# A convolution and whitening kernel: a DRAM buffer with rows p and 128+p of an image side by side

## The chip, the cores and the metric

The kernel runs on one core of a Trainium2 chip. The metric is device time in microseconds (us). Before the change, three runs gave 902.69, 903.47 and 903.47 us, median 903.47. A profiled execution is a run of its own; its span reaches from its first to its last instruction.

## The reference

The input x holds 4 images of 64 channels of 256 x 256 float32 pixels (67.1 MB). Two layers follow.

```
# layer 0: per channel a long 2-D convolution, kernel = outer product of two generated 1-D filters
k = einsum('ijk,imk->ijmk', hx, hy)
y = irfft2(rfft2(x, 512 x 512) * rfft2(k, 512 x 512) / 512)[..., :256, :256] + x * bias

# layer 1: whitening over the 64 channels
x1  = y as (64, 4*65536)
s   = x1[:, ::9]                       # every ninth pixel
mean = mean(s);  cov = s @ s.T / n + 0.01 * I
out = inverse_sqrt(cov, 5 Newton-Schulz steps) @ (x1 - mean)
```

The convolution is causal in both image directions and separable, so it is computed as two products with triangular Toeplitz matrices. The whitening matrix needs a sample of every image before the first output pixel can be made, so y has to be kept in full in the meantime: it goes out to DRAM and comes back.

## The kernel before

**First stage, the convolution.** The 64 channels are worked in groups of CG = 8; a step is one group g of one image n, 32 steps in all. The order of the steps is written out by hand (`steps`): the first six groups go through all four images, then the last two groups image by image, so that image 0 is complete after step 25, image 1 after step 27, and so on. A step's input sits in one of four tiles of [128 partitions, 8 channels, 2, 256], partition p holding the image rows p (index b = 0) and 128 + p (b = 1) of each channel. The tile is loaded two channels at a time (`load_x`, L101, 512 KB each) two steps ahead. `group` computes two channels' second product beside the next two channels' first one (L220, TensorE), ScalarE copies the first product out of PSUM (L409), VectorE adds the bias term and writes y over x in the tile (L412). Then `store` sends the two channels to DRAM (L425), in two transfers, one for each b, and VectorE picks the sample out of the tile (L319).

**The buffer in DRAM.** `y_d[n]` has H2 * C = 128 rows of 32768 floats: row b * 64 + channel, and in it the 128 image rows of half b one after another. A store of two channels and one b writes, from each of the 128 partitions, one run of 256 floats (1 KB) for each channel.

**The reload.** The last stage works in 32 pieces (n, q), eight for an image. A piece is a tile of [128, 4096], 2 MB: partition b * 64 + channel, 4096 consecutive floats of that row of `y_d[n]`. `load_y` (L357) loads it in one transfer of 128 runs of 16 KB. The tiles are placed, by the list `homes`, in thirteen buffers of the pools that the first stage leaves free; a piece's load waits until its buffer's earlier user is done. Nine loads are put by hand into the last steps of the first stage (`early`), the first after step 26's third quarter; four follow at its end. Piece i + 13 is loaded once the output store of piece i has left the buffer.

**Whitening.** After the last step the sample's covariance is summed (L333), and `whitening` computes the 64 x 64 matrix W and the shift: a short chain of small products.

**Last stage.** For each piece, four blocks: W times 64 partitions of 512 columns, four matmuls into two PSUM banks (L635), one bank evacuated by ScalarE (L639), the other by VectorE (L640), both in place over the piece's tile. The two column runs of a block lie 2048 apart (`v` splits the 4096 columns in two halves). Then the piece goes out (L645): piece 0 in four stores, piece 1 and the last two in two each, all others in one of 2 MB. GpSimd (POOL) issues the stores of pieces 1 to 18, SP those of piece 0 and of pieces 19 to 31. The order of pixels within the output tensor is settled on the host by a transpose.

**What sets the order.** Engines run their instructions in the order in which the kernel is written. SP issues nearly all transfers: x loads, Toeplitz loads (L193), y stores, y loads and some of the output stores, in one queue. A transfer that has to wait there, for a semaphore or for room, holds up all that is written behind it. Within a step SP's order for two channels is: y store, x load, Toeplitz load if any, y load if any.

Of the kernel before, what the change touches and what calls it, by code (L numbers as in the profile page):

```python
# [38 lines left out]
F32 = mybir.dt.float32  # L39
I32 = mybir.dt.int32  # L40
AF = mybir.ActivationFunctionType
ALU = mybir.AluOpType
# [3 lines left out]
NB, C, L = 4, 64, 256  # L46
P, H2 = 128, 2
EMB, ORDER = 33, 64
PIX = L * L
CG = 8  # L50
# [7 lines left out]
FP = 4096  # L58
# [6 lines left out]
def conv_whiten_kernel(ctx: ExitStack, tc: tile.TileContext, a: dict, out: bass.AP):  # L65
    nc = tc.nc
# [8 lines left out]
    dram = ctx.enter_context(tc.tile_pool(name="dram", bufs=1, space=bass.MemoryType.DRAM))  # L75
    psA = ctx.enter_context(tc.tile_pool(name="psA", bufs=8, space=bass.MemoryType.PSUM))

    y_d = [dram.tile([H2 * C, PIX // H2], F32, tag=f"y{n}", name=f"y_d{n}") for n in range(NB)]
    g_d = dram.tile([P, GW], F32, tag="g", name="g_d")
    g0_d = dram.tile([2 * CG, GW], F32, tag="g0", name="g0_d")  # L80

# [6 lines left out]
    cols = const.tile([P, 4], F32, tag="cols", name="cols")  # L88
# [9 lines left out]
    bias = const.tile([P, C], F32, tag="bias", name="bias")  # L98
# [22 lines left out]
    for n in range(NB):  # L121
        t = spool.tile([P, FP], F32, tag="samp", name=f"samp{n}")
# [32 lines left out]
    for i in range(3):  # L155
        for u in range(2):
# [3 lines left out]
            arg, k, nxt = (scratch[:, 2 + 3 * i + v, half] for v in range(3))  # L160
# [152 lines left out]
    def pack_ops(g, n, yt, cs):  # L313
        def op(s):
            nj = (L - s + STEP - 1) // STEP
            src = yt[:, cs, :, s : s + STEP * (nj - 1) + 1 : STEP].rearrange("p c b j -> p b j c")
            dst = samp[n][:, :, 0:nj, g * CG + cs.start : g * CG + cs.stop]
            m = mask[:, n, :, s : s + 1].unsqueeze(3).to_broadcast([P, H2, nj, cs.stop - cs.start])
            nc.vector.copy_predicated(dst, m, src)  # L319

        cost = 0.3 + 1.5e-3 * H2 * NJ * (cs.stop - cs.start)
        return [(cost, lambda s=s: op(s)) for s in range(STEP)]
# [21 lines left out]
    pieces = [(n, q) for n in range(NB) for q in range(PIX // H2 // FP)]  # L344
# [7 lines left out]
    def load_y(i):  # L352

        n, q = pieces[i]
        pool, tag = homes[i % len(homes)]
        t = pool.tile([P, FP], F32, tag=tag, name=f"yi_{n}_{q}")
        nc.sync.dma_start(out=t, in_=y_d[n][:, q * FP : (q + 1) * FP])  # L357
        return t

    def load_next():  # L360
        loaded[len(loaded)] = load_y(len(loaded))
# [10 lines left out]
    for g in range(1, C // CG):  # L372
        first = 16 * g - 14 if g < C // CG - 1 else 16 * g - 22
        for part in range(8):
            k = first + (part * 12 // 8 if g < C // CG - 2 else part)
# [18 lines left out]
    def group(first, second):  # L394

        units = []
        g1, n1, c1, x1, o1s1 = first
        g2, n2, c2, x2, o1s2 = second
        for u in range(2):
            job2 = (bank(f"p2_{g2}_{n2}_{c2 + u}"), o1s2[u], toep[g2][:, 1, c2 + u, :])  # L400
            job1 = (bank(f"p1_{g1}_{n1}_{c1 + u}"), x1[:, c1 + u], toep[g1][:, 0, c1 + u, :])
            units.append((job1, job2))

        toeplitz_products(units, orders[0])
        orders.reverse()
        for u in range(2):
            o1 = o1pool.tile([P, H2, L], F32, tag="o1", name=f"o1_{g1}_{n1}_{c1 + u}")
            for to, fr in ((slice(0, HP), slice(HP, P)), (slice(HP, P), slice(0, HP))):
                nc.scalar.copy(o1[to], units[u][0][0][fr])  # L409
            o1s1.append(o1)  # L410
            ch = g2 * CG + c2 + u
            nc.vector.scalar_tensor_tensor(  # L412
                x2[:, c2 + u], x2[:, c2 + u], bias[:, ch : ch + 1], units[u][1][0],
                ALU.mult, ALU.add,
            )

        store(second)
        pack(2.92)

    def store(second):  # L420
        g, n, c, yt, _ = second
        halves = g >= C // CG - 2
        for b in range(H2):
            row = b * C + g * CG + c
            nc.sync.dma_start(  # L425
                out=y_d[n][row : row + 2, :].rearrange("c (p w) -> p c w", w=L),
                in_=yt[:, c : c + 2, b],
            )

        if c == CG - 2 and (g, n) != steps[-1]:  # L430
            todo.extend(pack_ops(g, n, yt, slice(CG // 2 if halves else 0, CG)))
        elif c == CG // 2 - 2 and halves:
            todo.extend(pack_ops(g, n, yt, slice(0, CG // 2)))
# [123 lines left out]
    with tc.manual_schedule(  # L557
# [9 lines left out]
        for i, (g, n) in enumerate(steps):  # L567
            xt = x_tiles[i % 4]
            for c in range(0, CG, 2):
# [19 lines left out]
                if (i, c) in blocks:  # L589
                    tg, part = blocks[i, c]  # L590
# [6 lines left out]
        g, n, c, yt, _ = pending[0]  # L597
        for item in pending:
            half_group(item, 1)
            pack(1.0)  # L600
            store(item)
# [13 lines left out]
        W, shift = whitening(i15, ones)  # L615


    halves = [slice(u * C, (u + 1) * C) for u in range(2)]
    for i, (n, q) in enumerate(pieces):
        yt = loaded.pop(i)  # L620

        v = yt.rearrange("p (v f) -> p v f", v=2)
        o = out[n, q].rearrange("p (v f) -> p v f", v=2)

        part = 512 if i == 0 else 1024 if i == 1 or i > len(pieces) - 3 else 2048
        for w in range(FP // 1024):


            cols = slice(w * 512, (w + 1) * 512)
            po = [  # L630
                psA.tile([P, 512], F32, tag="psA", name=f"po_{n}_{q}_{w}_{u}") for u in range(2)
            ]
            for k in range(2):
                for u in range(2):
                    nc.tensor.matmul(  # L635
                        po[u][halves[k]], lhsT=W[halves[u]], rhs=v[halves[u], k, cols],
                        start=True, stop=True,
                    )
            nc.scalar.activation(v[:, 0, cols], po[0], AF.Identity, bias=shift)  # L639
            nc.vector.tensor_scalar(v[:, 1, cols], po[1], shift, None, ALU.add)  # L640
            end = (w + 1) * 512
            if end % part == 0:

                issue = nc.sync if i == 0 or i + len(homes) >= len(pieces) else nc.gpsimd
                issue.dma_start(out=o[:, :, end - part : end], in_=v[:, :, end - part : end])  # L645
        if i + len(homes) < len(pieces):
            loaded[i + len(homes)] = load_y(i + len(homes))

# [57 lines left out]
```

## Time and profile before

| | |
|---|---|
| median of three runs | 903.47 us |
| span of the profiled execution | 902.1 us |
| TensorE busy (matmul) | 781.2 us, 87% |
| VectorE, ScalarE, GpSimd busy | 64%, 44%, 2% |
| bytes moved by DMA | 285.6 MB, 317 GB/s over the span |
| read from HBM, written to HBM | 149.35 MB, 134.44 MB |
| chain that ended last: TensorE | 74% (64% of it the convolution's products, L220) |
| same chain: DMA, with the steps whose releaser isn't known | 11% and 7% |
| first and last y load issued (L357) | 507.7 us, 829.1 us |
| convolution's last product ends | about 613 us |
| first product of the last stage (L635) | 643.3 us |

An issue table lists transfers by the line that issues them, with their size in KB and the median time from issue to landing. A DMA packet is a run of bytes that one of the core's 16 DMA engines moves in one go; the trace records its start, its duration and its size. A busy share of the DMA engines is a mean over the sixteen: two full engines and fourteen idle ones would show as 0.13. The chain that ended last is followed back from the last instruction to what released it, step by step.

### The profile page before, as it was taken

The page shows a single profiled execution, that of the slowest core. Times are in us where ns is not written, and L with a number is a line of the kernel's source. Part 1 is how long each engine was busy: PE and PEld are TensorE (multiplying, and loading weights), DVE is VectorE, ACT ScalarE, POOL GpSimd, SP SyncE. Part 2 cuts the span into 40 slices and gives each one's busy share as a digit, 9 for nine tenths or more (in the row PEclk, how much of TensorE's full clock was granted, in tenths as well). Part 3 has the DMA queues.
Part 4 walks back from the last instruction along what each step waited for, and adds up shares of the span by engine and source line. Part 5 has one row for each costly group of instructions (what it writes and reads, how often), then busy time and mean ns, then how long its engine had stood idle before and what let it go on. Part 6 is the DMA issues. An engine that isn't in the chain of part 4 may idle for free.

```text
span 902.1 us, 28046 instructions
## 1 busy us (share of the span) xinstructions
PE 781.2 (87%) x11928; PEld 647.5 (72%) x11928; DVE 581.5 (64%) x801; ACT 395.5 (44%) x676; POOL 14.5 (2%) x40
## 2 busy tenths in 40 slices
PE   8999999999999999999999999999999565666200
PEld 7999999999999999999999999999533111212000
DVE  3487778877888778877888877877688332233200
ACT  2655554545455555545454444442487232233200
POOL 1000000000000000000000000000010000000000
PEclk9999999999999999999999999999999766866755
DMA  7988889798788888888997899979999999999998
GB/s 209 327 262 252 242 261 271 234 273 251 247 263 261 244 264 259 258 250 267 293 275 241 285 351 356 335 237 390 375 401 429 430 432 432 429 434 430 430 430 355
DMA packets 117912, 285.61 MB, mean 317 GB/s; under 512 B 8891, under 2 KB 91116, under 8 KB 110108
## 3 DMA queue, kind: packets, MB, share of 16 engines
q1 hardware_dynamic: 113436, 244.94, 79.0%
q0 software_dynamic: 3056, 37.95, 10.0%
q8 instruction: 95, 1.56, 0.7%
q10 hardware_dynamic: 1296, 0.93, 0.4%
q14 instruction: 29, 0.24, 0.1%
HBM read 149.35 MB, written 134.44 MB: 315 GB/s over the span
## 4 chain that ended last, share of the span: by engine, by line
PE 74%; DMA 11%; another core or an unknown queue 7%; DVE 0%; issue 0%; SPq 0%; ACT 0%; POOLq 0%; DVEq 0%
PE p L220 64%; DMA out_dram<-yi 5%; DMA yi<-y_d 5%; PE po L635 4%; PE pc L333 2%; PE ph L252 1%; PE pk L300 1%; PE spin L442 1%; DMA toep<-g_d 0%; PE busy L152 0%; PE pm L158 0%; SPq L357 0%; DMA scratch<-in_zw_dram 0%; DVE yi L640 0%
## 5 line engine op out<-in xcount | busy, mean ns | idle before, releaser
L220 PE MATMUL p<-toep,x 64*64 64x64 f32 (+3 forms) x5040 | 579.5, 284 | 0.8 <-issue 0.8
L220 PE MATMUL p<-toep,o 64*64 64x64 f32 (+3 forms) x5040 | 579.5, 284 | 0.0
L220 PEld LDWEIGHTS p<-toep,x 64*128 64x128 f32 (+1 forms) x5040 | 535.7, 166 | 24.4 <-issue 1.3
L220 PEld LDWEIGHTS p<-toep,o 64*128 64x128 f32 (+1 forms) x5040 | 536.7, 166 | 10.7 <-issue 0.2
L409 ACT COPY o<-p 64x512 f32<-64x512 f32 x504 | 292.8, 581 | 294.2 <-PE p L220 286.6
L319 DVE COPY_PREDICATED samp<-mask,x 128x464 f32<-128x464 int32 (+3 forms) x351 | 297.2, 847 | 9.8 <-DVE x L412 0.2
L412 DVE SCALAR_TENSOR_TENSOR x<-x,bias,p 128x512 f32<-128x512 f32 x252 | 179.8, 744 | 121.3 <-PE p L220 117.3
L635 PE MATMUL po<-yi,chain 64*64 64x512 f32 x1024 | 143.7, 720 | 60.4 <-DMA yi<-y_d 60.4
L640 DVE TENSOR_SCALAR yi<-po,shift 128x512 f32<-128x512 f32 x128 | 96.1, 751 | 109.0 <-PE po L635 100.7
L635 PEld LDWEIGHTS po<-yi,chain 64*64 64x64 f32 x1024 | 48.0, 162 | 155.2 <-issue 150.5
L639 ACT ACTIVATE yi<-po,shift 128x512 f32<-128x512 f32 x128 | 88.0, 687 | 116.7 <-PE po L635 116.0
L333 PE MATMUL pc<-samp 128*64 128x65 f32 x464 | 14.9, 223 | 0.0
L333 PEld LDWEIGHTS pc<-samp 128*64 128x64 f32 x464 | 14.3, 137 | 0.3
L645 POOL DMA_DIRECT2D out_dram<-yi x19 | 10.5, 554 | 130.5 <-DMA out_dram<-yi 55.1
L606 POOL TENSOR_SCALAR chain<-ident 64x64 f32<-64x64 f32 x2 | 1.0, 519 | 606.6 <-PE ph L252 606.6
L286 DVE COPY o<-ph 64x256 f32<-64x256 f32 x8 | 3.4, 422 | 9.7 <-PE ph L252 9.6
L152 PE MATMUL busy<-idle 128*128 128x128 f32 x64 | 9.4, 307 | 0.0
L152 PEld LDWEIGHTS busy<-idle 128*128 128x128 f32 x64 | 8.9, 222 | 0.2 <-issue 0.2
L300 PE MATMUL pk<-x,pick 128*128 128x56 f32 (+1 forms) x72 | 8.3, 292 | 0.0
L300 PEld LDWEIGHTS pk<-x,pick 128*128 128x128 f32 x72 | 8.1, 192 | 0.1
L442 PE MATMUL spin<-ident 128*128 128x128 f32 x50 | 7.9, 292 | 0.0
L286 ACT COPY o<-ph 64x256 f32<-64x256 f32 x8 | 2.9, 368 | 10.7 <-DMA toep<-g_d 9.2
(93 smaller groups left out, 77.4 us busy)
## 6 DMA issues: line engine op xcount, KB each, us to landing
x<-in_x_dram SPq DMA_DIRECT2D x128, 512.0 KB, 5.3
y_d<-x SPq DMA_DIRECT2D x256, 256.0 KB, 3.5
yi<-y_d SPq DMA_DIRECT2D x32, 2048.0 KB, 15.6
out_dram<-yi POOLq DMA_DIRECT2D x17, 2048.0 KB, 67.7
out_dram<-yi SPq DMA_DIRECT2D x11, 2048.0 KB, 32.9
toep<-g_d SPq DMA_DIRECT2D x28, 256.0 KB, 6.3
toep<-g_d SPq DMA_DIRECT2D x29, 192.0 KB, 5.7
out_dram<-yi SPq DMA_DIRECT2D x4, 1024.0 KB, 32.8
```

What stands on the lines that cost most here:

```text
L152: nc.tensor.matmul(p, lhsT=idle[:, 0:P], rhs=idle[:, P : 2 * P], start=True, stop=True)
L220: mm = nc.tensor.matmul(ps[q : q + w, m, HP * k : L], lhsT=src[parts, k // 2, m * P + q : m * P + q + w], rhs=t[parts, : stop : -1] if k e ...
L300: nc.tensor.matmul(pk[:, b, :, 0:nj], lhsT=pick[:, (s - b) % STEP, :], rhs=yt[:, cs, b, s : s + STEP * (nj - 1) + 1 : STEP], start=(s == 0 ...
L319: nc.vector.copy_predicated(dst, m, src)
L333: nc.tensor.matmul(pc[half], lhsT=samp[n][:, b, j, 0:C], rhs=samp[n][:, b, j, :], start=(b == 0 and j < 2), stop=(b == H2 - 1 and j >= NJ ...
L409: nc.scalar.copy(o1[to], units[u][0][0][fr])
L412: nc.vector.scalar_tensor_tensor(x2[:, c2 + u], x2[:, c2 + u], bias[:, ch : ch + 1], units[u][1][0], ALU.mult, ALU.add,)
L442: nc.tensor.matmul(p, lhsT=ident, rhs=ident, start=True, stop=True)
L635: nc.tensor.matmul(po[u][halves[k]], lhsT=W[halves[u]], rhs=v[halves[u], k, cols], start=True, stop=True,)
L639: nc.scalar.activation(v[:, 0, cols], po[0], AF.Identity, bias=shift)
L640: nc.vector.tensor_scalar(v[:, 1, cols], po[1], shift, None, ALU.add)
L645: issue.dma_start(out=o[:, :, end - part : end], in_=v[:, :, end - part : end])
```

## The change

`y_d[n]` now has a row for each of the 64 channels, 65536 floats long, and in it, for each p, the 256 pixels of image row p and then the 256 of row 128 + p. A store of two channels is one transfer with runs of 512 floats (2 KB). A piece still has 128 partitions of 4096 floats; partition h * 64 + channel now holds floats from half h of the channel's row, which is read with a hand-built access pattern: 2 halves with a step of 32768 elements, 64 channels with a step of 65536, 4096 elements. In the last stage a block is 1024 consecutive columns, and stores cover consecutive columns; the host's transpose follows.

```diff
-    y_d = [dram.tile([H2 * C, PIX // H2], F32, tag=f"y{n}", name=f"y_d{n}") for n in range(NB)]
+    y_d = [dram.tile([C, PIX], F32, tag=f"y{n}", name=f"y_d{n}") for n in range(NB)]
...
-        nc.sync.dma_start(out=t, in_=y_d[n][:, q * FP : (q + 1) * FP])
+        nc.sync.dma_start(
+            out=t,
+            in_=bass.AP(
+                tensor=y_d[n].tensor,
+                offset=y_d[n].offset + q * FP,
+                ap=[[PIX // H2, H2], [PIX, C], [1, FP]],
+            ),
+        )
...
-        for b in range(H2):
-            row = b * C + g * CG + c
-            nc.sync.dma_start(
-                out=y_d[n][row : row + 2, :].rearrange("c (p w) -> p c w", w=L),
-                in_=yt[:, c : c + 2, b],
-            )
+        row = g * CG + c
+        nc.sync.dma_start(
+            out=y_d[n][row : row + 2, :].rearrange("c (p w) -> p c w", w=H2 * L),
+            in_=yt[:, c : c + 2].rearrange("p c b w -> p c (b w)"),
+        )
...
-        v = yt.rearrange("p (v f) -> p v f", v=2)
-        o = out[n, q].rearrange("p (v f) -> p v f", v=2)
-
-        part = 512 if i == 0 else 1024 if i == 1 or i > len(pieces) - 3 else 2048
+        v = yt.rearrange("p (w v f) -> p w v f", v=2, f=512)
+
+        part = 1024 if i == 0 else 2048 if i == 1 or i > len(pieces) - 3 else 4096
...
-                        po[u][halves[k]], lhsT=W[halves[u]], rhs=v[halves[u], k, cols],
+                        po[u][halves[k]], lhsT=W[halves[u]], rhs=v[halves[u], w, k],
...
-            nc.scalar.activation(v[:, 0, cols], po[0], AF.Identity, bias=shift)
-            nc.vector.tensor_scalar(v[:, 1, cols], po[1], shift, None, ALU.add)
-            end = (w + 1) * 512
+            nc.scalar.activation(v[:, w, 0], po[0], AF.Identity, bias=shift)
+            nc.vector.tensor_scalar(v[:, w, 1], po[1], shift, None, ALU.add)
+            end = (w + 1) * 1024
...
-                issue.dma_start(out=o[:, :, end - part : end], in_=v[:, :, end - part : end])
+                issue.dma_start(out=out[n, q][:, end - part : end], in_=yt[:, end - part : end])
```

More of the change, by code (lines that the diff above doesn't have):

```diff
@@ L620, in conv_whiten_kernel @@
         yt = loaded.pop(i)
-        v = yt.rearrange("p (v f) -> p v f", v=2)
-        o = out[n, q].rearrange("p (v f) -> p v f", v=2)
-        part = 512 if i == 0 else 1024 if i == 1 or i > len(pieces) - 3 else 2048
+        v = yt.rearrange("p (w v f) -> p w v f", v=2, f=512)
+        part = 1024 if i == 0 else 2048 if i == 1 or i > len(pieces) - 3 else 4096
         for w in range(FP // 1024):
-            cols = slice(w * 512, (w + 1) * 512)
             po = [
@@ L702 @@
     r = run_bass_kernel_spmd(nc, [arrays], core_ids=[0])
-    y = np.asarray(r.results[0]["out_0_dram"]).reshape(NB, PIX // H2 // FP, H2, C, H2, FP // 2)
-    return np.ascontiguousarray(y.transpose(0, 3, 4, 1, 2, 5)).reshape(NB, C, L, L)
+    y = np.asarray(r.results[0]["out_0_dram"]).reshape(NB, PIX // H2 // FP, H2, C, FP // 1024, H2, H2, L)
+    return np.ascontiguousarray(y.transpose(0, 3, 6, 5, 1, 4, 2, 7)).reshape(NB, C, L, L)
```

## The prediction

> **What bounds the kernel now.** I read the windows by stage first, then the DMA queue in the last stage, then what SP (the queue that issues nearly every transfer) waits for and how its issues stand in time. The windows' columns are the stretch, its length, the busy us (and instructions) of PE, PEld, DVE, ACT and POOL, the granted clock, the mean busy share of the 16 DMA engines, and GB/s.
>
> ```profile
> 22.50:513.00 490.50, 490.13 (x8525) 461.43 (x8524) 381.76 (x469) 251.88 (x439) 0.00 (x0) 1.00 0.86 262
> 513.00:643.00 130.00, 128.35 (x2240) 120.23 (x2237) 96.08 (x180) 48.89 (x94) 1.15 (x3) 1.00 0.92 344
> 643.00:686.00 43.00, 43.00 (x403) 15.42 (x405) 36.49 (x49) 33.70 (x50) 6.25 (x11) 1.00 0.97 387
> 686.00:829.00 143.00, 89.15 (x550) 29.01 (x546) 51.38 (x69) 46.96 (x69) 4.28 (x8) 0.75 1.01 430
> 829.00:902.00 73.00, 11.69 (x84) 3.69 (x76) 8.26 (x11) 7.56 (x11) 0.00 (x0) 0.59 0.96 408
> ```
>
> Up to 686 us PE is never free; DMA is at 0.86 to 0.97. From 686 on the DMA engines are full and PE is not: the last stage is a copy at 430 GB/s. The next view is the DMA answer for 700 to 850 us, and below it the issue table (KB of one transfer, median us from issue to landing).
>
> ```profile
> DMA packets 4436, 64.51 MB, mean 430 GB/s; under 512 B 498, under 2 KB 498, under 8 KB 498
> ```
>
> ```profile
> y_d<-x SPq DMA_DIRECT2D x256, 256.0 KB, 3.5
> yi<-y_d SPq DMA_DIRECT2D x32, 2048.0 KB, 15.6
> ...
> g_d<-scratch POOLq DMA_DIRECT2D x1, 192.0 KB, 2.3
> ...
> scratch<-in_zw_dram SPq DMA_DIRECT2D x1, 49.5 KB
> ...
> g_d<-scratch ACTq DMA_DIRECT2D x1, 12.0 KB
> g_d<-scratch SPq DMA_DIRECT2D x1, 12.0 KB
> ```
>
> 4436 - 498 = 3938 packets of 16 KB in 150 us on 16 engines: 150 x 16 / 3938 = 0.609 us for one 16 KB row on one engine (26.9 GB/s). The packet records give the same in the median, 0.611 us, and 0.608 at the least of 5504: an engine does not go faster, however empty the others are. I use 0.611.
>
> Three transfers in that table have no landing time, and this is the line that decides the case. The landing is read where a transfer's semaphore has had sixteen steps from the DMA engines. In the semaphore record the POOL store of 128 rows (g_d) has sixteen such steps; the two 12 KB stores, which walk 8 rows, have eight (12.27 to 12.44 us for SP's), and the 33-row load has eleven (2.35 to 2.58 us). 8 rows were carried by 8 engines, 33 rows by 11, the largest number up to 16 that divides the count. So a transfer is dealt out along its slowest dimension, in equal parts.
>
> ```profile
> SPq L425 <- DVE x L412: 323.3, 125, 6.5
> SPq L357 <- DMA out_dram<-yi: 171.4, 20, 9.9
> ```
>
> ```profile
> 829.56 50.16 SPq L645 DMA_DIRECT2D out_dram<-yi  x14
> ```
>
> SP's waits: in the long first part it waits for DVE's results, so it has time over; in the last part for buffers. The timeline line shows its last 14 issues spread over 50.16 us, one per 4.9 us at the end: SP's queue is in order and takes a new transfer only as the engines drain the old ones, some 39 us deep by the issue-to-landing time of the last of them.
>
> **The change part by part.** (1) *Two y stores become one* (L425): 256 issues of 256 KB become 128 of 512 KB, rows of 1 KB become 2 KB. Nothing else moves: PE, ACT, DVE and POOL keep their instructions in order, SP loses 128. An issue costs 0.4 us of SP (the two stores of a pair start 0.4 to 0.5 us apart), 128 x 0.4 = 51 us of an engine that waited 323 us for DVE. Worth 0: the cover is that wait and PE's full stage. On the engines a 1 KB row took 0.053 us (100 to 400 us), so a 512 KB store is 32 x 0.053 = 1.7 us per engine now; as 2 KB rows it lies between that and 32 KB at 26.9 GB/s = 1.2 us. Before 507 us that is hidden under PE; if PE's cover were gone it would be a gain of at most 128 x 0.5 = 64 us.
>
> (2) *Last pass in blocks of 1024*: the same 1024 matmuls of 64x512, 128 ACT and 128 DVE instructions on runs of 512 elements that stay contiguous. 0. *Its stores*: the split stores' rows grow from 2 and 4 KB to 4 and 8 KB. 4 KB rows ran at 25.8 GB/s per engine (0.159 us), 16 KB rows at 26.8: 4% of 8 MB / 430 GB/s = 19.5 us is 0.8 us at most. I take 0.4 us gained and neglect it below.
>
> (3) *The y load* (L357). Its source was 128 rows with one step, slowest count 128. It becomes a list of three: 2 halves, 64 channels, 4096 elements. The steps (32768, then 65536) do not merge into one count of 128. The slowest count of the source is now 2; the destination's is 128. By the 8-row and 33-row transfers a part is an equal share of the slowest count, and a count of 2 has two parts. So 64 rows of 16 KB go to each of two engines: 64 x 0.611 = 39.1 us per load, against 8 x 0.611 = 4.9 us. No transfer of before has two sides with unlike counts where the smaller is under 16, so this is bounded: 39.1 us if the smaller side decides, 4.9 us if the 128 side does. I take 39.1: an equal deal of a source of two parts to sixteen engines would need the second dimension cut, and nothing in the trace cuts one (the 33-row load used 11 engines, not 16). [...]
>
> **The sum** goes by the work of those two engines, which bound the kernel from the first y load on. That load is issued at 507.7 us (first L357 start) and nothing ahead of it changes. Each load holds the two engines 39.1 us, and the first nine are issued 4 to 26 us apart, so they never run dry. Each then has to do:
> - 32 loads x 39.1 = 1251 us
> - its sixteenth of 32 output pieces, 8 rows each: 32 x 8 x 0.611 = 156
> - 13 x loads still to come (issue times after 507.7), 8 rows of 4 KB: 13 x 8 x 0.159 = 16
> - 23 merged y stores to come, 1.2 to 1.7 us: 33
> - two places where SP waits for a landing with its queue empty: load 6 (L357) takes the x buffer of step 29, whose last stores lie behind load 5; load 13 takes the buffer of piece 0, whose stores SP issues behind load 12. About 3 us each, from the 2.3 us landing of a small store: 6
> - the first nine loads run beside the products; there a 16 KB packet took 0.672 us in the mean (510 to 640 us): 9 x 64 x 0.061 = 35 at most. The rest of the traffic will be thinner, so I take 5
> - end of the last packet (900.4) to the end of the span (902.1): 2
>
> 507.7 + 1251 + 156 + 16 + 33 + 6 + 5 + 2 = 1977 us of span. The profiled span of before is 902.1 beside a median of 903.5, so the time is 1978 us.
>
> What is late next: SP's queue is in order, so x loads and y stores behind a y load wait for the two slow engines. PE stands for the first time near step 29, whose second x quarter lies behind loads 0 and 1 (507.7 + 78 + 5 = 591 us, instead of about 558). Load 4 precedes the last two quarters of step 31: 507.7 + 5 x 39.1 + about 12 of other rows = 715 us, so the products end some 120 us later than 613, and the whitening near 765. None of this adds to the sum: the two engines work through it. In the last pass POOL's stores slip in beside the loads; from piece 19 on the stores are SP's and stand behind load 31, so 13 pieces x 4.9 = 64 us of plain stores at full width end the run.
>
> **The rivals.** *A: the load stays on sixteen engines* (the destination's 128 decides). For it: all 32 loads of before did so with this destination. Against: the 8- and 33-row transfers. It decides from a landing time near 16 us on. Then the last stage is the same 430 GB/s copy, the split stores give 0.4 us, and the 23 late y stores 23 x (0 to 0.5) = 0 to 11 us of engine time, which only counts where DMA is full: from 0.92 busy in 513 to 643, say a quarter. 903.5 - 0.4 - 2 = 901 us (898 to 903.5): faster or no change.
>
> *B: sixteen engines, but rows now 256 KB apart instead of 128 KB cost.* No row shows a stride that costs; the slowest 16 KB packets on record are the 0.672 us above: 19 loads after 643 us x 8 x 0.061 = 9, so 912 us. [...]
>
> *C: two engines, and they run dry between loads.* If every load waited for the one before, 32 x 2.3 (the 192 KB store's landing) = 74 us: 1978 + 74 - 6 = 2046 us. Against it: the 14 queued issues above, back to back. It is the top of my range.
>
> *D: one engine*, if the count-1 dimension that the destination gained were split: 508 + 32 x 128 x 0.611 + 211 + 13 = 3235 us. The 256-row output stores of before carry such a dimension too and landed with sixteen steps.
>
> **How the numbers follow.** Two engines: 0.90 (C within it 0.06). A: 0.07, of which faster 0.05 and no change 0.02. B 0.02, D 0.01. A difference under 0.2% (1.8 us) could not be told from none. Forecast 1978 us. Low end: without the 33 of y stores and the 5, should those fall into moments when the two engines wait: 1940. High end: 35 instead of 5 for the packets beside the products, and C's 74 instead of 6: 2076, and a little for a late start, 2090. Cases outside hold about 0.15. Faster 0.05, same 0.02, slower 0.93.
>
> **What would show it.** Right: y loads land some 40 us or more after issue instead of 15.6; their semaphores step from two engines; SP spends hundreds of us inside L357's issues or waits; in the last pass one load per about 44 us (39.1 + 4.9), that is (2.1 + 2.1) MB / 44 = 95 GB/s instead of 430, with a DMA share near 2/16 + 14/16 x 4.9/44 = 0.22; PE waits for y loads; a last stretch of some 64 us back at 430 GB/s. The products end late, near 735 us. Wrong: landings near 16 us, DMA share near 1 after 690, a time near 900. If the loads hold 39 us each but the time is over 2090, the gaps are mis-sized; if PE's stage ends at 613 still, the in-order reading of SP's queue is.

## The result, and the profile after

The changed kernel takes 1977.13 us in the median (1976.75 to 1977.21, four runs) beside 903.08 us for the kernel before: a ratio of 2.190, 95% interval 2.187 to 2.193. The profiled execution spans 1975.3 us.

The windows by stage of the changed kernel, columns as in the prediction (stretch, length, busy us of PE, PEld, DVE, ACT, POOL, granted clock, DMA share, GB/s):

```profile
22.50:513.00 490.50, 490.19 (x8548) 461.24 (x8548) 381.49 (x469) 251.42 (x438) 0.00 (x0) 1.00 0.82 261
513.00:735.00 222.00, 99.37 (x1736) 93.15 (x1727) 74.41 (x120) 41.77 (x72) 0.00 (x0) 0.72 0.30 106
...
1100.00:1905.00 805.00, 109.83 (x608) 34.25 (x608) 57.09 (x76) 52.26 (x76) 3.73 (x7) 0.56 0.20 86
```

Up to the first y load nothing has changed but the DMA share (0.82 for 0.86, the merged store). Then both TensorE and the DMA engines are mostly idle, and that is the mark of this case: a share of 0.20 is two engines full and fourteen that carry a store now and then. The mean hides the two.

The y load's own line in the changed kernel (issue durations min/median/max, first and last start), and who waited for it:

```profile
L357 SPq DMA_DIRECT2D yi<-y_d x32: 492/25429/83467, 506.6 to 1828.1; - x32
...
  PE po L639: 961.3, 26
```

Issuing a y load took SP 25.4 us in the median; before it was 0.32 us. TensorE waited 961 us for y loads in the last pass (60.4 us before). The issue table:

```profile
y_d<-x SPq DMA_DIRECT2D x128, 512.0 KB
yi<-y_d SPq DMA_DIRECT2D x32, 2048.0 KB
out_dram<-yi POOLq DMA_DIRECT2D x17, 2048.0 KB, 14.3
```

Like the 8-row and 33-row transfers of before, the y loads have no landing time. In the semaphore record load 0, issued at 506.6 us, has two steps from the DMA engines, at 551.8 and 552.7 us, 45 us after its issue. SP's other transfers share their semaphores with y loads, which takes the landing from them too.

The waits by engine show how long TensorE stood for x loads, and the timeline of SP shows why:

```profile
PE p L220 <- DMA x<-in_x_dram: 135.1, 5, 35.5
```

```profile
506.60 0.60 SPq L357 DMA_DIRECT2D yi<-y_d  x1
509.93 0.39 SPq L431 DMA_DIRECT2D y_d<-x  x1
510.37 4.38 SPq L101 DMA_DIRECT2D x<-in_x_dram  x1
514.85 0.38 SPq L431 DMA_DIRECT2D y_d<-x  x1
515.28 19.64 SPq L101 DMA_DIRECT2D x<-in_x_dram  x1
535.01 6.17 SPq L357 DMA_DIRECT2D yi<-y_d  x1
541.27 13.06 SPq L431 DMA_DIRECT2D y_d<-x  x1
```

The second column is how long SP was in the instruction. An x load that is issued in 0.4 us elsewhere takes 19.64 us behind y load 0. The landings show two engines behind the rest: in the semaphore record the y store issued at 562.7 us has fourteen of its sixteen steps between 570.4 and 572.3 us and the last two at 600.5 and 602.0. That the issue itself waits for room on those two is the author's reading; no view shows it.

### The profile page after: what moved, and what is told of

Same layout as the page of the kernel before. It is cut to its first block, busy times and chain, and to the rows that moved or that the text cites. A ratio compares the mean times of both kernels' runs of the same rounds, so it can differ in the third digit from the quotient of the medians.

```text
span 1975.3 us, 27888 instructions
## 1 busy us (share of the span) xinstructions
PE 820.6 (42%) x11928; PEld 664.1 (34%) x11928; DVE 581.8 (29%) x801; ACT 395.1 (20%) x676; POOL 14.1 (1%) x40
## 4 chain that ended last, share of the span: by engine, by line
another core or an unknown queue 48%; PE 37%; DMA 12%; DVE 0%; issue 0%; DVEq 0%; SPq 0%
PE p L220 26%; PE po L639 9%; DMA x<-in_x_dram 7%; DMA yi<-y_d 2%; DMA y_d<-x 2%; PE ph L252 1%; PE pk L300 0%; PE spin L448 0%; PE busy L152 0%; DMA toep<-g_d 0%; PE pc L333 0%; PE pm L158 0%; DMA scratch<-in_zw_dram 0%; DMA g_d<-scratch 0%
## 5 line engine op out<-in xcount | busy, mean ns | idle before, releaser
L220 PE MATMUL p<-toep,x 64*64 64x64 f32 (+3 forms) x5040 | 590.6, 288 | 135.4 <-DMA x<-in_x_dram 135.1
L220 PEld LDWEIGHTS p<-toep,x 64*128 64x128 f32 (+1 forms) x5040 | 545.6, 169 | 160.3 <-issue 136.4
L220 PE MATMUL p<-toep,o 64*64 64x64 f32 (+3 forms) x5040 | 591.0, 288 | 0.0
L639 PE MATMUL po<-yi,chain 64*64 64x512 f32 x1024 | 171.2, 830 | 961.3 <-DMA yi<-y_d 961.3
L220 PEld LDWEIGHTS p<-toep,o 64*128 64x128 f32 (+1 forms) x5040 | 546.7, 169 | 10.9 <-issue 0.2
L639 PEld LDWEIGHTS po<-yi,chain 64*64 64x64 f32 x1024 | 54.1, 189 | 1077.7 <-issue 1077.0
L448 PEld LDWEIGHTS spin<-ident 128*128 128x128 f32 x50 | 6.3, 191 | 0.5
L252 PE MATMUL ph<-toep,x 64*128 64x192 f32 (+3 forms) x64 | 6.0, 327 | 0.8 <-DMA toep<-g_d 0.8
```

The costliest lines, as they stand in the source:

```text
L220: mm = nc.tensor.matmul(ps[q : q + w, m, HP * k : L], lhsT=src[parts, k // 2, m * P + q : m * P + q + w], rhs=t[parts, : stop : -1] if k e ...
L252: mm = nc.tensor.matmul(ps[m][:, HP * k : L], lhsT=src[parts, k // 2, m * P : (m + 1) * P], rhs=t[parts, : stop : -1] if k else t[parts, : ...
L448: nc.tensor.matmul(p, lhsT=ident, rhs=ident, start=True, stop=True)
L639: nc.tensor.matmul(po[u][halves[k]], lhsT=W[halves[u]], rhs=v[halves[u], w, k], start=True, stop=True,)
```

## The experiments

All medians are in us; the kernel before, measured beside them, gave 902.7 to 903.0.

| run | what differs | median | ratio to before (95%) |
|---|---|---|---|
| two_loads | changed kernel, load in two transfers | 979.5 | 1.084 (1.081 to 1.087) |
| count2_alone | kernel before, source list 2 x 64 | 1976.7 | 2.189 (2.185 to 2.193) |
| count8 | changed kernel, list 8 x 16 | 1171 (1141 and 1201) | |
| count16 | changed kernel, list 16 x 8 | 988.9 | 1.095 (1.092 to 1.098) |
| before_halves | kernel before, load in two transfers | 985.5 | 1.092 (1.089 to 1.094) |
| every_second | two_loads, every second partition | 907.1 | 1.006 (1.004 to 1.008) |
| one_list | changed kernel, one list of 128 rows | 901.4 | 0.9988 (0.9979 to 0.9997) |
| count16_back | kernel before, list 16 x 8 | 997.0 | 1.104 (1.100 to 1.109) |
| no_early | changed kernel, no y load before the last step | 2029.5 | 2.248 (2.244 to 2.252) |
| store_count2 | kernel before, 11 stores to a list 2 x 64 | 1280.5 | 1.418 (1.415 to 1.421) |
| blocks_alone | kernel before, last pass in blocks of 1024 | 902.0 | 0.9993 (0.9984 to 1.0002) |

### Is it the list, and its first count?

Three theories are tested here. Theory 1 is the prediction's: a transfer is dealt to the largest number of engines, up to 16, that divides the slowest count of both sides; it is read from the semaphore steps of before (8 for 8 rows, 11 for 33, 16 for 128), and no transfer there shows it for two unlike sides with the smaller under 16. Theory 2: rows that lie far apart, or the new layout in memory, are read slowly. Theory 3: a source list of three levels is slow, whatever its counts.

The edit of count2_alone, the kernel before with the changed kernel's access pattern on its own buffer:

```diff
-        nc.sync.dma_start(out=t, in_=y_d[n][:, q * FP : (q + 1) * FP])
+        nc.sync.dma_start(out=t, in_=bass.AP(tensor=y_d[n].tensor, offset=y_d[n].offset + q * FP,
+                                             ap=[[PIX // H2, H2], [PIX, C], [1, FP]]))
```

> The kernel before with nothing but the y load's source list changed to 2, 64 and 4096 elements (the channels' order in the piece is another, so the output is permuted); two y stores, old layout in memory, old blocks. Theory 1: the two engines' work is 507.7 + 1251 + 156 + 16 (x) + 23 x 32 x 0.053 = 39 (y stores as 1 KB rows) + 6 + 5 + 2 + 1.3 = 1984 us (1960 to 2010): the whole loss sits in this one list. Theory 2 in its form that the layout in memory is to blame: near 903 us. Theory 3: near 1980 us.

Measured 1976.7 us: the whole loss, to 0.1%, with the old buffer, the old stores and the old last pass. The new layout in memory is not needed for it.

The edits of count8 and count16 change two numbers of the list in the changed kernel (k is 8 or 16):

```diff
-                ap=[[PIX // H2, H2], [PIX, C], [1, FP]],
+                ap=[[PIX // H2, k], [k * PIX // H2, P // k], [1, FP]],
```

> The changed kernel with the y load's source list as 16, 8 and 4096 elements: still three levels (the output is permuted), an engine's rows 2 MB apart. Theory 1: 16 engines, 4.9 us a load, 901 us (898 to 910). Theory 2: slower than with 256 KB, over 1000 us. Theory 3: near 1977 us.

> The changed kernel with the y load's source list as 8, 16 and 4096 elements: three levels as before, same bytes, rows dealt in another order (the output is permuted). Theory 1: 8 engines, 16 rows each, 9.8 us a load. The first thirteen loads (127 us) lie between 507 and about 655 us; from load 13 on 19 x 9.8 + 32 x 4.9 = 343 us: about 1000 us (970 to 1040). Theory 2 with the rows of one engine 1 MB apart: as slow as now or slower, 1977 us or more. Theory 3: near 1977 us.

Both fall far below 1977 us with the same three levels and the same bytes, so theory 3 (three levels are slow as such) is out, and the first count sets the order: 2 gives 1977, 8 some 1140 to 1200, 16 989 us. But both miss theory 1's number. count16 lies 88 us over 901; count8 about 140 to 200 us over 1000 (its two runs lie 5% apart, so only the rough size of that counts). Something besides the number of engines costs here.

The same in the repair that lay nearest, two transfers of 64 rows each:

```diff
+        for h in range(H2):
+            nc.sync.dma_start(
+                out=t[h * C : (h + 1) * C],
+                in_=y_d[n][:, h * (PIX // H2) + q * FP : h * (PIX // H2) + (q + 1) * FP],
+            )
```

> The changed kernel with each y load as two transfers, one for each half h: 64 rows of 16 KB on both sides, still 256 KB apart in memory, y stores and last pass as changed. Theory 1 (a transfer is dealt to the largest number of engines up to 16 that divides the slowest count of both sides): 64 and 64 give 16 engines, a load is back at 8 x 0.611 = 4.9 us of each engine, landing near 16 us, DMA full after 690 us; 901 us (898 to 906). Theory 2 (rows 256 KB apart, or the new layout in memory, read slowly): unchanged, near 1977 us. Theory 3 (a source list of three levels is slow whatever its counts): near 901 us.

979 us: neither 901 nor 1977. Theory 2 asked for no change and is out as the cause of the 1977. What is left over shows in the DMA view of two_loads for 870 to 960 us, forty slices of 2.25 us, in which the last loads end and the stores follow:

```profile
GB/s 233 218 226 218 226 211 233 211 211 226 233 211 218 233 204 233 226 197 248 291 335 422 422 430 430 444 437 415 451 422 415 444 437 408 444 437 437 415 451 422
```

While loads alone run it is 220 GB/s with all engines busy, then 430 with stores alone. In the packet records a load's 16 KB took 1.18 us in the mean between 510 and 640 us (1.17 in count16), where before it took 0.672, with a median of 0.611.

### Half the rate with sixteen engines: where it reads or where it writes?

before_halves cuts the load of the kernel before in the same way (`out=t[h * C : (h + 1) * C]`, `in_=y_d[n][h * C : (h + 1) * C, ...]`); rows stay 128 KB apart.

> The kernel before with nothing but each y load cut into two transfers, partitions 0 to 63 and 64 to 127, rows 128 KB apart as ever. two_loads came to 979 us, its 16 KB load packets at 1.18 us instead of 0.611, and the question is why. Theory P (where it writes: sixteen engines that all write partitions of one half get half the rate): the same loss, 965 to 990 us, load packets near 1.2 us. Theory H (where it reads: rows 256 KB apart or more are read at half the rate): nothing lost, 903 to 906 us, packets near 0.62 us.

985.5 us. The DMA share and GB/s of before_halves while loads are queued:

```profile
829.00:902.00 73.00, 47.32 (x244) 16.04 (x248) 21.78 (x29) 19.94 (x30) 0.00 (x0) 0.71 1.01 246
```

All engines busy, 246 GB/s, packets at 1.18 us between 510 and 640: half the rate without any change in what is read.

every_second changes in two_loads only the partitions that a transfer writes:

```diff
-                out=t[h * C : (h + 1) * C],
+                out=t[h::2],
```

> two_loads with nothing changed but the partitions that a transfer writes: half h goes to partitions h, h + 2, h + 4 and so on instead of 64 in a row (the output is permuted). Rows are 256 KB apart as in two_loads. Theory P: both halves of the partitions are written at once, packets at 0.62 us, 898 to 910 us. Theory H: as two_loads, 975 to 985 us.

907.1 us, packets at 0.612 us from 690 us on, rows still 256 KB apart. The windows of every_second:

```profile
686.00:829.00 143.00, 83.65 (x516) 27.09 (x508) 48.58 (x66) 44.46 (x65) 3.73 (x7) 0.76 1.01 426
```

So reading rows 256 KB apart cost nothing that shows in the packets (0.612 us beside 0.611; theory H is out; the 4 us that are left over the kernel before, 0.4 to 0.75%, no run explains), and sixteen engines that wrote 64 neighbouring partitions together got half the rate (theory P): 220 to 246 GB/s in two_loads and before_halves beside 426 in every_second and 430 before. Why neighbouring partitions take longer, no run shows.

count16 lost as much, and its transfers write all 128 partitions. count16_back takes a list of the same counts to the kernel before, over the rows that this kernel always read:

> The kernel before with the y load's list as 16, 8 and 4096 elements, the eight rows of each group taken backwards so that the list keeps three levels (the output is permuted); by theory 1 an engine still reads the same eight rows as before. Theory H: 903 to 908 us. Theory P, if a list of three levels gives an engine eight partitions in a row, of which sixteen engines together write only a half at any time: 975 to 995 us, load packets near 1.2 us, as in count16.

```diff
+                offset=y_d[n].offset + 7 * (PIX // H2) + q * FP,
+                ap=[[8 * PIX // H2, 16], [-PIX // H2, 8], [1, FP]],
```

997 us (993 and 1001, at the top of theory P's range and over it), packets at 1.17 us in the mean between 510 and 640. The same 128 rows are read, all 128 partitions are written, and still it is half the rate. Theory P's condition, that a list of three levels gives an engine eight partitions in a row, would fit; the records don't tell which engine read which rows or wrote which partition, so it is not shown. Shown is that it isn't the set of rows that a transfer reads. count8's miss looks the same: in its profile (of the 1201 us run) the 16 KB packets took 0.98 us in the mean between 510 and 640.

### What the rest of the change is worth

one_list gives the y load of the changed kernel its single list of 128 rows back:

```diff
-                ap=[[PIX // H2, H2], [PIX, C], [1, FP]],
+                ap=[[PIX // H2, P], [1, FP]],
```

> The changed kernel with the y load's source as one list of 128 rows of 16 KB, 128 KB apart, as before the change (a partition holds half p % 2 of channel p // 2, so the output is permuted). What is left of the change is the merged y store and the last pass in blocks of 1024. Theories P and H: 901 us (898 to 904), the price of the rest of the change: 0 to 5 us gained. Against both: if the merged store or the new blocks cost, over 905 us.

901.4 us, 0.12% under the kernel before (0.03 to 0.21%). Its last stage is that of before again, and the landing time is back; windows and issue table of one_list:

```profile
686.00:829.00 143.00, 87.55 (x540) 28.50 (x536) 50.08 (x68) 45.81 (x68) 4.26 (x8) 0.77 1.01 430
```

```profile
yi<-y_d SPq DMA_DIRECT2D x32, 2048.0 KB, 16.1
```

It is no version to use: a partition holds half p % 2 of channel p // 2, while the last pass multiplies 64 neighbouring partitions that have to be one half's channels.

> The kernel before with the last pass in blocks of 1024 consecutive columns alone; y stores, buffer and y load as before, the host's transpose to match. one_list came to a ratio of 0.9988 with the merged store and the blocks. If the longer rows of the split output stores are the gain (0.4 us worked out, 0.8 at most): 902.3 us (901.9 to 902.7), a ratio of 0.9991 to 1. If the merged store is the gain: no difference, 902.7 us.

902.0 us, a ratio whose interval holds 1. The blocks cost nothing and may give the 0.4 us; which of the two parts makes one_list's 0.12% stays open. No version here that can be used beats the kernel before by a difference that the runs can tell.

### Does the sum hold, and which side counts?

no_early sets `early = {}`, so that all y loads come after the last step.

> The changed kernel with no y load put into the first stage: all 32 come after the last step. In the changed kernel the products stood 135 us for x loads that wait behind y loads, and that is now gone. By the sum (the two engines' work decides, the products' delay adds nothing) the time is the first load's start, near 621 us, + 1251 + 156 + 3 for one gap + 2 + 1.3 = 2034 us (2010 to 2070): slower than the changed kernel though its products end 135 us earlier. Rival: the products' delay is part of the time; then it is faster than the changed kernel, 1840 to 1900 us.

2029.5 us, 52 us slower than the changed kernel, though its products end at their old time. Windows of no_early:

```profile
513.00:643.00 130.00, 126.63 (x2196) 118.58 (x2190) 95.48 (x179) 48.65 (x94) 1.14 (x3) 1.00 0.44 150
643.00:686.00 43.00, 5.49 (x32) 1.76 (x32) 3.00 (x4) 2.75 (x4) 0.00 (x0) 0.58 0.13 54
```

TensorE isn't held up any more (126.63 of 130 us, against 99.37 of the 222 us after 513 above), and the first product of the last pass starts at 662 us instead of 789. All of that is lost again: a DMA share of 0.13 is two engines of sixteen, and they started at 619 instead of 507.

store_count2 gives the 2 MB stores of SP in the kernel before a destination list with a first count of 2 (the lines that are added):

```diff
+                        out=bass.AP(tensor=out.tensor, offset=out[n, q].offset,
+                                    ap=[[FP, H2], [H2 * FP, C], [1, FP]]), in_=yt,
```

> The kernel before with the eleven 2 MB output stores that SP issues (pieces 19 to 29) written through a destination list of 2, 64 and 4096 elements; the source in the tile stays 128 partitions (the output rows are permuted). Theory 1, both sides count: two engines, 39.1 us each; from the first of them at 820 us, 820 + 11 x 39.1 + 4 x 2.5 + 5 + 2 + 1.3 = 1268 us (1250 to 1290). Rival, only the list of the source counts: 903 us.

1280.5 us. The timeline of SP and the windows of store_count2:

```profile
830.80 349.20 SPq L646 DMA_DIRECT2D out_dram<-yi  x10
```

```profile
902.00:1260.00 358.00, 0.00 (x0) 0.00 (x0) 0.00 (x0) 0.00 (x0) 0.00 (x0) 0.50 0.15 64
```

Ten issues take 349 us, at a share of 0.15. Here the source is 128 partitions and the destination's first count is 2: the time is that of two engines (2/16 is 0.125), so the smaller count decided on the writing side as well. No tile is written here, so which partitions are written has no part in it.

## Why the prediction was right

**What bounds it.** Right: from the first y load on, two engines, by the two semaphore steps of a y load. count2_alone, count8 and count16 (1976.7, 1171 and 988.9 us) tie it to the list's first count, store_count2 (1280.5 us) to either side. That the smaller of two unlike counts decides was the prediction's choice, which nothing in the trace of before shows; the two steps and the times of count2_alone and store_count2 show it.

**The price of a load**, 39.1 us. Right: the 16 KB packets kept a median of 0.611 us. By the semaphore record y loads landed 43.8 us apart while POOL's stores ran beside them (1223.5, 1267.3, 1311.1, 1354.9), where 44 was predicted, and 39.0 to 39.1 apart once those stores were through (1598.4, 1637.5, 1676.5, 1715.5). An engine was no faster for the others' idleness (0.608 us at the least, as before), and with two of them at work the loss of the sixteen-engine runs (1.18 us) doesn't show.

**The sum.** 1977 us of span predicted, 1975.3 measured; 1978 and 1977.1 in time. The start came 1.1 us earlier (506.6 for 507.7), the rest holds to 0.6 us. So close a fit is in part luck: of the 6 us for two waits the packet records show 1.8 us without a packet, at 1132 us, so the other terms together were some 4 us short. In no_early the same terms gave 2034 for 2029.5. That the products' delay adds nothing was the boldest step, and no_early shows it.

**The edits at nothing** (one y store, blocks of 1024). Right: one_list measures them together at 0.03 to 0.21% gained.

**What is late next.** The mechanism was right, the size short: the first stall ended at 601 us where 591 was worked out, and the last pass began 146 us later (789.4 for 643.3) where some 120 was said. The term that was too small is the "about 12 of other rows" beside the first five y loads. The x load that TensorE waited for last was issued at 697.5 us and landed at 747.4, where 715 was worked out. By then SP had issued twelve x loads and twelve y stores since load 0; at the prediction's own prices (1.3 and 1.4 us of an engine) that is some 32 us. The 16 KB packets, at 0.64 us in the mean between 510 and 640, make up some 9 us more (5 x 64 x 0.029).

**The end.** Wrong in its picture: not 64 us of stores at full width. The DMA view of the changed kernel for 1800 to 1976 us, forty slices of 4.4 us:

```profile
GB/s 52 60 52 52 52 56 264 261 52 52 60 52 52 52 56 56 365 447 439 216 261 451 436 425 365 52 261 425 417 419 255 216 264 261 52 56 56 48 56 19
```

After 1870 us bursts of up to 451 GB/s stand between stretches at 48 to 56, and at 1826 to 1835 stores already ran at some 260. So the fourteen free engines did part of their share while the two still loaded. Load 31 landed at 1915.7 us; the two engines had some 58 us of stores left after it. Their own work was counted rightly, so the sum didn't suffer.

**Rivals.** A's number (901 us) is that of one_list, so its working was right; its condition was too weak, since two_loads, count16 and count16_back have sixteen engines and lose 76 to 94 us. B foresaw a loss at sixteen engines and blamed the distance between rows; every_second shows that this distance cost the packets nothing (0.612 us). C and D didn't happen: from the first y load to the end of the stores fewer than two packets were on the way for those 1.8 us and for no other stretch over 0.3 us, and a load's semaphore has two steps from the DMA engines, not one.

## What to carry to other kernels

Read a transfer's access patterns as the list of counts that they are: here a harmless-looking halves-by-channels reordering with a 2 in front, on one side alone, put a 2 MB load on two engines and made it take 39.0 us of them instead of 4.9 us of sixteen, eight times as long; stores with a 2 in front of their destination ran at 52 to 57 GB/s from 900 to 1185 us (store_count2), where the loads had 54. Then look at the tile's side: a transfer to 64 neighbouring partitions used all engines here (a share of 1.01) and ran at half the rate, 1.18 us for 16 KB. In the profile of the changed kernel a DMA share of 0.20 next to a queue whose issue instruction took 25.4 us in the median was the sign of a transfer on few engines; what was queued behind it paid too, an x load up to 19.64 us for its issue instead of 0.4.

## What the runs showed of the hardware

- Sixteen engines that wrote 64 neighbouring partitions together (two_loads, before_halves; a DMA share of 1.01): 1.18 us for 16 KB and 220 to 246 GB/s, against 0.611 us and 430 before; every second partition instead (every_second): 0.612 us and 426 GB/s.
- A source list of three levels with a first count of 16 and all 128 partitions written ran at that half rate too (1.17 us in count16 and count16_back; 989 and 997 us).
- In the changed kernel the issue of a y load, whose semaphore steps from two engines, took SP 25.4 us in the median (0.32 before). Behind y loads the issue of an x load took up to 19.6 us and that of a y store up to 54.6 us, 512 KB each.
- A y load of the changed kernel, source list first count 2, into 128 partitions, has two steps of its semaphore from the DMA engines; with no stores beside them y loads landed 39.0 to 39.1 us apart, at 54 GB/s. The same list in the layout of before gave the same time (1976.7 beside 1977.1 us).
